# A graph layer's last 24 edge blocks: messages in halves, queued behind dense work, and dense work paced

## The chip, the cores and the metric

The kernel runs on one core of a Trainium2 chip. A core has five engines that work side by side, each through its own queue in order: TensorE (PE; matmuls; its weight loads are PEld in the profile), VectorE (DVE), ScalarE (ACT), GpSimd (POOL, which here only starts gathers) and SyncE (SP, which here only starts other transfers). The metric is the device time of one execution in microseconds (us); lower is better.

## The reference

A graph network layer over 8192 nodes with 256 channels and 131072 edges with 64 features. Edges come sorted by their destination.

```python
ea = edge_attr @ w_e + b_e
msg = relu(x[src] + ea)
agg = segment_sum(msg, dst, num_segments=N)
t = x + agg
h_local = bn(relu(t @ w1 + b1) @ w2 + b2 + x)
# attention with 4 heads inside groups of 32 nodes, on x
h_attn = bn(attention(x) + x)
out = h_local + h_attn
out = bn(out + relu(out @ m_w1 + m_b1) @ m_w2 + m_b2)
return layernorm(x + out)
```

All is float32. The edge part (`msg`, `agg`) and the attention depend on x alone; the dense part (w1, w2, m_w1, m_w2, layer norm) of a node needs the sums of all its edges.

## The kernel before, in words

**Edges** go in 128 blocks of 1024. A block is four groups (`NH`) of two columns of 128 edges (`TJ`). Its steps, with their lines:

- `gather` (L157): eight indirect DMAs on POOL, 128 rows of x each, into one of four buffers `xs`.
- `edge_products` (L208): edge features times w_e on PE. Each pair of groups (half a block) fills one tile `pe` of two PSUM banks; there are two such tiles, and the attention scores (L474) take the same two in turn.
- `edge_messages` (L229, L233): for each half, DVE adds `pe` and the gathered rows, then ACT takes the relu. There are three `msg` buffers.
- `edge_hot` (L241): one-hot columns of each edge's destination inside its group's window of 32 nodes, on DVE.
- `edge_sums` (L250, L263): PE sums messages by destination into tile `pw` (one buffer), ACT copies the sums to `ws`, DVE makes a second one-hot `oh2` (L267).
- `edge_place` (L278, L287): PE spreads the window sums over some 100 to 160 nodes, into a tile that shares the buffer of `pw`, and DVE adds them to the chunk's `xT`.
- `next_edges` (L190): DVE transposes the features of the block after next, and SP loads further ones.

**Nodes** go in 16 chunks of 512. `attention_front` and `attention_back` compute a chunk's attention ahead of time; `dense` (the layers at L546, the relus on ACT at L553 and L562, the scaled additions on DVE at L556 and L574, transposes at L583, layer norm at L589 to L601, the store at L606) starts when the last block that reaches the chunk has been placed. They are Python generators which yield after each step, with the step's cost in us as the writer estimates it. The second to last chunk's dense part goes in two halves, the last chunk's in four quarters of 128 nodes, on two streams.

**Order.** PE runs in the order in which the program states its matmuls. The order on DVE and ACT is chosen by a scheduler, except that `tc.issue_after(i)` puts what is stated inside it behind instruction `i` on the same engine. Up to block 103 two blocks go per round, with shares of dense work between. From block 104 (`TAIL`) a planner states the steps one by one. It keeps an estimated clock `t`; `came[i]` is the time at which it expects block i's gathers, `7.9 + 10.035 * (i + 1)`. In each turn it takes the first of these that is due: placing a block, its sums, products of the next block, messages; if none is due, `work.step` states one dense or attention step. Messages of a block stand behind the newest `ws` copy and the newest addition to `xT`. Products of a block come after the messages of the block before; the last block's two halves of products are stated by hand, one after the sums of block 126 and one after its placement.

Of the kernel before, what the change touches and what calls it, by code (L numbers as in the profile page):

```python
# [18 lines left out]
P = 128  # L19
# [5 lines left out]
NH = 4  # L25
# [16 lines left out]
TAIL = 104  # L42
AGG_ROWS = N + 2 * P
# [29 lines left out]
def gnn_kernel(ctx: ExitStack, tc: tile.TileContext, x, src, dst, edge_attr, w, out):  # L73
# [119 lines left out]
    pe_of, msg_of, oh_of, newest = {}, {}, {}, {}  # L193
# [25 lines left out]
    def edge_messages(b):  # L219

        xs = xs_of.pop(b)
        msg = msg_of[b] = epool.tile([P, NH, TJ, C], FP, name="msg", tag="msg", bufs=3)
        n = 2 if b < NB - 1 else 1
        for h in range(0, NH, 2):
            pe = pe_of.pop((b, h))
            for u in range(0, 2, n):
                hs = slice(h + u, h + u + n)
                for js in [slice(0, TJ)] if n == 2 or h + u < NH - 1 else [slice(j, j + 1) for j in range(TJ)]:
                    nc.vector.tensor_add(  # L229
                        msg[:, hs, js].rearrange("p u i c -> p i u c"), pe[:, js, u : u + n, :],  # L230
                        xs[:, hs, js].rearrange("p u i c -> p i u c"),
                    )
                    nc.scalar.activation(msg[:, hs, js], msg[:, hs, js], AF.Relu)  # L233
        between()
# [19 lines left out]

    def edge_sums(blocks):

        n = len(blocks)
        pw = pps.tile([P, 2, C], FP, name="pw", tag="pw", bufs=1)
        for i, b in enumerate(blocks):
            turns = [(h, j) for j in range(TJ) for h in range(NH)]  # L260
            group_sums(pw, i, b, sorted(turns) if b == NB - 1 else turns)
        ws = epool.tile([P, 2, C], FP, name="ws", tag="ws", bufs=2)
        newest["ws"] = nc.scalar.copy(ws[:, :n], pw[:, :n]).ins  # L263
# [269 lines left out]
    def dense(n0, st, pool, bank, a=0, z=CH, own=("h1", "m1", "zT", "y", "")):  # L533
# [18 lines left out]
        for o in range(KC):  # L552
            nc.scalar.activation(h1[:, o, :], layer(w1, KC, o, tT), AF.Relu, bias=v_("b1", o))  # L553
            yield 1.7 * part
        for o in range(KC):
            nc.vector.scalar_tensor_tensor(  # L556
                hA[:, o, :], layer(w2, KC, o, h1), s1[:, o : o + 1], hA[:, o, :], op0=ALU.mult, op1=ALU.add
            )
            yield 1.7 * part
        m1 = pool.tile([P, 2 * KC, w], FP, name="m1", tag=own[1])  # L560
        for o in range(2 * KC):
            nc.scalar.activation(m1[:, o, :], layer(mw1, KC, o, hA), AF.Relu, bias=v_("m_b1", o))  # L562
            yield 1.7 * part
# [9 lines left out]
        for o in range(KC):  # L573
            nc.vector.scalar_tensor_tensor(  # L574
                zT[:, o, :], layer(mw2, 2 * KC, o, m1), s3[:, o : o + 1], zT[:, o, :], op0=ALU.mult, op1=ALU.add
            )
# [66 lines left out]
    class Work:  # L643
# [5 lines left out]
        def __init__(self, n):  # L649
            self.streams = [[] for _ in range(n)]  # L650
            self.rest, self.turn, self.owed = [0] * n, 0, 0.0
            self.at, self.placed_at = [0.0] * n, 0.0

# [56 lines left out]
    with tc.manual_schedule(engines={PE}):  # L710
# [23 lines left out]
        for i, c, a, z in (  # L734
            (DENSE2, NCH - 2, 0, CH // 2), (DENSE, NCH - 2, CH // 2, CH), (DENSE2, NCH - 1, 0, P),
# [56 lines left out]
        t, p, m, s, l = came[b - 2] + 20, b, b, b - 2, b - 2  # L792
        added = dict((i, came[i] + 2.0) for i in range(b))
        summed_at, bank_free = {}, t
        work.at = [t] * len(work.streams)
        while l < NB:

            times = [1e9] * 4
            if l < s:
                times[0] = summed_at[l] + 1.5  # L800
            elif s < m:
                times[1] = max(added[s] + 1.2, bank_free)
                if s == NB - 1:
                    times[1] = max(came[s] + 2.2, bank_free)
            if p < NB - 1 and m == p:
                times[2] = added[p - 1]
            if m < p:
                times[3] = came[m]
            if t >= times[0]:
                edge_place(*sums)  # L810
                placed = l
                t += 0.75
                bank_free = work.placed_at = t + 0.7
                l += 1
                if l == NB - 1:
                    edge_products(l, [2])
                    edge_hot(l)
                    t += 1.0
                    p += 1
            elif t >= times[1]:  # L820
                sums = edge_sums([s])
                t += 1.2
                summed_at[s] = t
                s += 1
                if s == NB - 1:
                    edge_products(s, [0])
                    t += 1.0
            elif t >= times[2]:
                if p + 2 < NB:
                    gather(p + 2)  # L830
                edge_products(p)
                next_edges(p + 2)
                edge_hot(p)
                t += 2.1
                p += 1
            elif t >= times[3]:

                with ExitStack() as behind:
                    for i in newest.values():
                        behind.enter_context(tc.issue_after(i))  # L840
                    edge_messages(m)
                added[m] = max(t, came[m], added[m - 1] + 0.5) + 2.0
                m += 1
            elif l == s - 1 == NB - 1:
                t = times[0]
# [127 lines left out]
```

## Time and profile before

| what | value |
|---|---|
| median of 3 runs | 1315.99 us (1314.24 to 1318.11) |
| the profiled execution | 1315.85 us, span of its instructions 1314.1 us |
| PE busy | 1198.9 us (91%) |
| POOL busy | 975.3 us (74%), with 0.3 us to issue between two gathers |
| DVE, ACT busy | 803.9 us (61%), 592.0 us (45%) |
| last gather starts | 1289.26 us |
| last operation on DVE starts | 1309.12 us |
| mean TensorE clock granted | 0.964 of full speed |

How to read it: a timeline row gives start, length, engine, line, operation, output and inputs, how many instructions are merged, and in brackets the idle time of the engine ahead of it with what ended that. A windows row gives a stretch, its length, and for PE, PEld, DVE, ACT and POOL the busy us and the number of instructions, then the granted TensorE clock, the share of the DMA engines and GB/s. A waits row names who waited for whom, with the sum in us and the number of times. Every matmul on float32 shows as two rows of PE. Line numbers are those of the kernel before.

### The profile page before, as it was taken

How to read it: one execution, taken by the hardware profiler on the slowest of the kernel's cores; microseconds unless marked ns; L12 is line 12 of the kernel's file. 1: busy time of each engine (PE TensorE's matmuls, PEld its weight loads, DVE VectorE, ACT ScalarE, POOL GpSimd, SP SyncE). 2: the span in 40 equal slices, each digit the busy share in tenths (PEclk: the TensorE clock that was granted, in tenths of full speed). 3: DMA queues.
4: the chain of work that ended last, by engine and by line, in shares of the span. 5: the costliest groups of instructions: out<-in, count | busy, mean ns of one | idle time of the engine just before them, and what ended most of it. 6: DMA issues, size and time to landing. Idle time of an engine off the chain costs nothing.

```text
span 1314.1 us, 21073 instructions
## 1 busy us (share of the span) xinstructions
PE 1198.9 (91%) x7683; PEld 722.8 (55%) x7683; DVE 803.9 (61%) x1634; ACT 592.0 (45%) x850; POOL 975.3 (74%) x1032
## 2 busy tenths in 40 slices
PE   5987989999999989898997999889898999989986
PEld 3554646556565555555564555545555555555665
DVE  6567665757566565745746574565647558475663
ACT  2524444454545264443544444354454445453443
POOL 7777777777777777777777777777777777777772
PEclk8989999999999989898999999989899999999998
DMA  9999976677666666665767566576566567665741
GB/s 230 280 328 275 280 216 166 175 188 192 169 182 158 171 181 159 188 163 152 195 163 185 153 185 169 154 186 169 169 170 191 149 168 194 162 168 154 193 135 48
DMA packets 148922, 240.35 MB, mean 183 GB/s; under 512 B 27950, under 2 KB 112204, under 8 KB 148044
## 3 DMA queue, kind: packets, MB, share of 16 engines
q0 software_dynamic: 49152, 134.28, 38.6%
q1 hardware_dynamic: 98572, 104.65, 29.4%
q8 instruction: 62, 1.02, 0.3%
q14 instruction: 48, 0.39, 0.1%
q10 hardware_dynamic: 1088, 0.00, 0.0%
HBM read 222.06 MB, written 16.78 MB: 182 GB/s over the span
## 4 chain that ended last, share of the span: by engine, by line
POOL 34%; PE 31%; issue 16%; DMA 9%; DVE 8%; ACT 2%; SPq 0%; DVEq 0%; POOLq 0%; ACTq 0%
POOL xs L157 34%; PE at L546 8%; DMA xs<-xb,srci 6%; PE pe L208 6%; PE at L443 3%; PE pw L250 3%; PE pe L203 2%; PE at L524 2%; DVE msg L229 2%; PE l L278 1%; DVE bd L504 1%; PE at L512 1%; PE at L457 1%; DMA xb<-xp 1%; DVE eaT L190 1%
## 5 line engine op out<-in xcount | busy, mean ns | idle before, releaser
L157 POOL DMA_INDIRECT xs<-xb,srci x864 | 819.1, 948 | 263.2 <-issue 247.7
L233 ACT ACTIVATE msg<-msg 128x1024 f32<-128x1024 f32 (+1 forms) x259 | 270.0, 1046 | 401.4 <-DVE msg L229 397.4
L229 DVE TENSOR_TENSOR msg<-pe,xs 128x1024 f32<-128x1024 f32 (+1 forms) x259 | 306.6, 1207 | 196.5 <-PE pe L208 91.2
L208 PE MATMUL pe<-we,eaT 64*128 64x256 f32 x2048 | 270.3, 401 | 13.5 <-ACT pr L484 9.8
L208 PEld LDWEIGHTS pe<-we,eaT 64*128 64x128 f32 x2048 | 195.4, 194 | 117.9 <-issue 62.8
L157 POOL DMA_INDIRECT xs<-in_x_dram,srci x144 | 138.8, 964 | 43.9 <-issue 40.8
L250 PE MATMUL pw<-msg,oh 128*32 128x256 f32 x2048 | 129.8, 385 | 1.2 <-ACT msg L233 0.8
L546 PE MATMUL at<-hA,mw 128*128 128x512 f32 (+2 forms) x320 | 125.8, 520 | 4.5 <-DVE hA L556 4.3
L443 PE MATMUL at<-xT,inT 128*128 128x512 f32 x256 | 121.8, 602 | 3.2 <-ACT xT L433 3.2
L546 PE MATMUL at<-m,mw 128*128 128x512 f32 (+2 forms) x320 | 119.4, 517 | 0.0
L190 DVE STREAM_TRANSPOSE eaT<-ea 128x512 f32<-128x512 f32 x128 | 90.0, 703 | 22.0 <-PE pe L208 18.6
L250 PEld LDWEIGHTS pw<-msg,oh 128*32 128x32 f32 x2048 | 59.9, 110 | 63.6 <-issue 22.8
L278 PEld LDWEIGHTS l<-oh,ws 128*128 128x128 f32 x512 | 73.7, 195 | 27.3 <-issue 21.4
L278 PE MATMUL l<-oh,ws 128*128 128x160 f32 (+4 forms) x512 | 85.9, 308 | 1.8 <-ACT ws L263 1.7
L546 PEld LDWEIGHTS at<-hA,mw 128*128 128x128 f32 x320 | 55.1, 192 | 53.4 <-issue 41.2
L546 PEld LDWEIGHTS at<-m,mw 128*128 128x128 f32 x320 | 55.7, 192 | 48.0 <-issue 44.8
L443 PEld LDWEIGHTS at<-xT,inT 128*128 128x128 f32 x256 | 46.9, 191 | 57.4 <-issue 47.6
L446 ACT ACTIVATE qk<-at,vec 128x512 f32<-128x512 f32 x64 | 43.8, 685 | 73.7 <-PE at L443 73.6
L546 PE MATMUL at<-xT,w 128*128 128x512 f32 (+2 forms) x160 | 66.3, 551 | 8.8 <-DVE xT L287 8.8
L562 ACT ACTIVATE m<-at,vec 128x512 f32<-128x512 f32 (+2 forms) x80 | 47.9, 599 | 58.5 <-PE at L546 58.0
L546 PE MATMUL at<-h,w 128*128 128x512 f32 (+2 forms) x160 | 65.3, 532 | 9.4 <-ACT oT L519 7.0
L241 DVE TENSOR_TENSOR oh<-iota_n,rel 128x128 f32<-128x128 f32 x256 | 57.6, 279 | 18.2 <-PE pw L250 14.8
(111 smaller groups left out, 1200.7 us busy)
## 6 DMA issues: line engine op xcount, KB each, us to landing
ea<-in_edge_attr_dram SPq DMA_DIRECT2D x512, 128.0 KB
xs<-xb,srci POOLq DMA_INDIRECT x864
xn<-in_x_dram SPq DMA_DIRECT2D x16, 512.0 KB
out_dram<-y SPq DMA_DIRECT2D x14, 512.0 KB
xp<-in_x_dram SPq DMA_DIRECT2D x10, 512.0 KB
xb<-xp SPq DMA_DIRECT2D x10, 512.0 KB
xp<-in_x_dram SPq DMA_DIRECT2D x3, 1024.0 KB
xb<-xp SPq DMA_DIRECT2D x3, 1024.0 KB
```

The source lines that it names most:

```text
L157: nc.gpsimd.indirect_dma_start(out=xs[:, h, j, :], out_offset=None, in_=x if b < NX else xb[:, :], in_offset=bass.IndirectOffsetOnAxis(ap= ...
L190: nc.vector.transpose(eaT, ea[:, QR:].rearrange("p (g d) -> p g d", d=ED)[:, :, :QR])
L208: nc.tensor.matmul(pe[:, i, u, :], eaT[rows, h + u], we[rows, :], start=(b >= NX), stop=True, skip_group_check=True)
L229: nc.vector.tensor_add(msg[:, hs, js].rearrange("p u i c -> p i u c"), pe[:, js, u : u + n, :], xs[:, hs, js].rearrange("p u i c -> p i u c"),
L233: nc.scalar.activation(msg[:, hs, js], msg[:, hs, js], AF.Relu)
L241: nc.vector.tensor_tensor(oh[:, ts], iota_n[:, None, :WN].to_broadcast([P, TB // 2, WN]), rel[:, b, ts, None].to_broadcast([P, TB // 2, WN ...
L250: nc.tensor.matmul(pw[h * WN : (h + 1) * WN, i, :], oh_of[b][:, h * TJ + j, :], msg_of[b][:, h, j, :], start=(j == 0), stop=(j == TJ - 1), ...
L278: nc.tensor.matmul(l2[:, k, at : at + wn], ws[:, i, k * P : (k + 1) * P], oh2[:, i, :wn], start=(i == 0 and k == 0), stop=(i == last), ski ...
L443: nc.tensor.matmul(ps, inT[:, k, o * P : (o + 1) * P], xT[:, k, :], start=(k == 0), stop=(k == KC - 1))
L446: nc.scalar.activation(qk[:, o, :], ps, AF.Identity, bias=v_("in_b", o))
L546: nc.tensor.matmul(ps, wt[:, k, o * P : (o + 1) * P], act[:, k, :], start=(k == 0), stop=(k == nk - 1))
L562: nc.scalar.activation(m1[:, o, :], layer(mw1, KC, o, hA), AF.Relu, bias=v_("m_b1", o))
```

## The change

It touches the last 24 blocks alone, with five edits.

1. Products, messages and sums go by halves of a block. The planner keeps for each of the three which block and which half is next; products of half k of a block become due when the message of half k of the block before is expected to be added. The first half of a block's sums can be stated before its second half's messages. The last block goes the same way; its sums go as three groups and then one.
2. Dense work is added to what messages stand behind: the newest relu (L553, L562) on ACT and the newest scaled addition (L556, L574) on DVE. The attention's own scaled addition isn't among them.
3. Between the expected times of block 115 and block 124 (`came[115]` to `came[124]`), dense and attention steps are stated only as credit allows, which grows by 0.42 us per us.
4. The second half of chunk 14's dense part goes as two quarters.
5. The planner's estimates change: shorter times for placements and sums, and an order of turns in which messages come ahead of products.

```diff
+SHARE = 0.42
...
-    def edge_messages(b):
+    def edge_messages(b, pairs=range(0, NH, 2)):
...
-        for h in range(0, NH, 2):
+        for h in pairs:
...
+    def some_sums(b, groups):
+
+        if b not in pw_of:
+            pw_of[b] = pps.tile([P, 2, C], FP, name="pw", tag="pw", bufs=1)
+        group_sums(pw_of[b], 0, b, [(h, j) for h in groups for j in range(TJ)])
...
-            nc.scalar.activation(h1[:, o, :], layer(w1, KC, o, tT), AF.Relu, bias=v_("b1", o))
+            newest["relu"] = nc.scalar.activation(h1[:, o, :], layer(w1, KC, o, tT), AF.Relu, bias=v_("b1", o)).ins
...
-            nc.vector.scalar_tensor_tensor(
+            newest["dense"] = nc.vector.scalar_tensor_tensor(
...
         def step(self, t, until):
 
+            if self.paced_from <= t < self.paced_to:
+                self.credit += SHARE * (t - max(self.seen, self.paced_from))
+                self.seen = t
+                if self.credit < -0.02:
+                    return min(until, t - self.credit / SHARE)
...
                     elif d > 0:
                         t += d
+                        if self.paced_from <= t:
+                            self.credit -= d
...
-            (DENSE2, NCH - 2, 0, CH // 2), (DENSE, NCH - 2, CH // 2, CH), (DENSE2, NCH - 1, 0, P),
+            (DENSE2, NCH - 2, 0, CH // 2), (DENSE, NCH - 2, CH // 2, 3 * P), (DENSE, NCH - 2, 3 * P, CH),
+            (DENSE2, NCH - 1, 0, P),
...
+        p, m, s = [b, 0], [b, 0], [b - 2, 0]
+        added = dict(((i, k), came[i] - 1.2 + 2.5 * k) for i in range(b) for k in range(2))
...
+        work.paced_from, work.paced_to = came[115], came[124]
...
+            if p[0] < NB and (p[0] - 1, p[1]) < tuple(m):
+                times[2] = added[p[0] - 1, p[1]]
+            if tuple(m) < tuple(p):
+                times[3] = came[m[0]] - 2.5 * (1 - m[1])
...
             elif t >= times[3]:
 
                 with ExitStack() as behind:
                     for i in newest.values():
                         behind.enter_context(tc.issue_after(i))
-                    edge_messages(m)
...
+                    edge_messages(m[0], (2 * m[1],))
+                added[tuple(m)] = max(t, came[m[0]] - 2.5 * (1 - m[1])) + 1.3
+                onward(m)
+            elif t >= times[2]:
+                i, k = p
+                if not k and i + 2 < NB:
+                    gather(i + 2)
+                edge_products(i, (2 * k,))
+                if k:
+                    next_edges(i + 2)
+                else:
+                    edge_hot(i)
+                t += 1.0
+                onward(p)
```

More of the change, by code (lines that the diff above doesn't have):

```diff
@@ L190, in edge_transpose @@
         nc.vector.transpose(eaT, ea[:, QR:].rearrange("p (g d) -> p g d", d=ED)[:, :, :QR])
-    pe_of, msg_of, oh_of, newest = {}, {}, {}, {}
+    pe_of, msg_of, oh_of, pw_of, newest = {}, {}, {}, {}, {}
     def edge_products(b, pairs=range(0, NH, 2)):
@@ L561, in dense @@
         for o in range(2 * KC):
-            nc.scalar.activation(m1[:, o, :], layer(mw1, KC, o, hA), AF.Relu, bias=v_("m_b1", o))
+            newest["relu"] = nc.scalar.activation(m1[:, o, :], layer(mw1, KC, o, hA), AF.Relu, bias=v_("m_b1", o)).ins
             yield 1.7 * part
@@ L573, in dense @@
         for o in range(KC):
-            nc.vector.scalar_tensor_tensor(
+            newest["dense"] = nc.vector.scalar_tensor_tensor(
                 zT[:, o, :], layer(mw2, 2 * KC, o, m1), s3[:, o : o + 1], zT[:, o, :], op0=ALU.mult, op1=ALU.add
-            )
+            ).ins
             yield 3.4 * part
@@ L811, in gnn_kernel @@
                 placed = l
-                t += 0.75
+                t += 0.6
                 bank_free = work.placed_at = t + 0.7
                 l += 1
[L815 to L819, printed above, removed]
-            elif t >= times[1]:
[L821 to L835, printed above, removed]
+            elif t >= times[1]:
+                i, k = s
+                last = range(NH - 1, NH) if i == NB - 1 else range(NH // 2, NH)
+                some_sums(i, last if k else range(last.start))
+                t += 0.14 * TJ * (len(last) if k else last.start)
+                if k:
+                    sums = edge_sums([i])
+                    summed_at[i] = t
+                onward(s)
             elif t >= times[3]:
```

45 lines of the change are left out of this document (22 added, 23 removed).

## The prediction

> **What bounds the kernel now.** I read the page first, then the windows over the last 250 us, then the timelines of POOL, DVE and PE there, and last the waits.
>
> ```profile
> span 1314.1 us, 21073 instructions
> PE 1198.9 (91%) x7683; PEld 722.8 (55%) x7683; DVE 803.9 (61%) x1634; ACT 592.0 (45%) x850; POOL 975.3 (74%) x1032
> ```
>
> The profiled execution took 1315.85 us, 1.75 us more than its span; the median of the three runs is 1315.99, so the sum below stands for the median as well.
>
> POOL sets a floor. Its gathers follow each other without a stall to the last:
>
> ```profile
> 1288.01 0.95 POOL L157 DMA_INDIRECT xs<-xb,srci  x1 [0.30 <-issue]
> 1289.26 0.94 POOL L157 DMA_INDIRECT xs<-xb,srci  x1 [0.30 <-issue]
> 1286.75 3.00 DMA xs<-xb,srci
> ```
>
> 0.95 + 0.30 us a gather, eight to a block, is 10.0 us a block, and the last one lands at about 1289.26 + 3.0 = 1292.3. Nothing in the diff makes a gather cheaper or earlier. So the change can only act on the 22 us behind 1292, or push what stands there back.
>
> ```profile
> 1064.00:1130.00 66.00, 62.45 (x434) 35.82 (x436) 44.65 (x92) 31.85 (x49) 49.97 (x53) 1.00 0.67 178
> 1130.00:1200.00 70.00, 65.83 (x414) 38.28 (x407) 44.68 (x89) 32.03 (x49) 53.03 (x56) 1.00 0.62 166
> 1200.00:1250.00 50.00, 47.10 (x316) 31.94 (x316) 32.01 (x71) 20.26 (x34) 37.90 (x40) 1.00 0.69 174
> 1250.00:1289.00 39.00, 32.71 (x259) 24.33 (x256) 23.55 (x52) 16.54 (x31) 29.51 (x32) 0.93 0.48 132
> 1289.00:1314.00 25.00, 16.72 (x131) 13.87 (x130) 9.26 (x26) 9.21 (x24) 0.94 (x1) 0.91 0.09 26
> ```
>
> The columns are the stretch, its length, and busy us of PE, PEld, DVE, ACT and POOL. PE is busy 175.4 of the 186 us from 1064 to 1250 (94%): in the last 24 blocks the bound is PE, not POOL. It is behind the gathers there, and catches up only at the end:
>
> ```profile
> 1148.88 0.95 POOL L157 DMA_INDIRECT xs<-xb,srci  x1 [0.31 <-issue]
> 1161.81 2.34 DVE L229 TENSOR_TENSOR msg<-pe,xs 128x1024 f32<-128x1024 f32 x2
> 1272.19 1.23 DVE L229 TENSOR_TENSOR msg<-pe,xs 128x1024 f32<-128x1024 f32 x1 [1.70 <-DMA xs<-xb,srci]
> ```
>
> Counting eight gathers and two messages to a block, the first two rows belong to block 113: its last rows landed near 1152, its messages ran ten us later. At block 125 (third row) DVE waits for the landing: the lag is gone. So PE has just enough room to reach the last gather without a backlog. PE idle time added before 1250 is not hidden by POOL; it arrives at the end, less what the waits of the last blocks give back.
>
> **The change part by part.** Matmul work is the same: 8 products, 8 sums, 2 placements a block, the same dense columns. What moves is who stands behind whom.
>
> *Halves.* Products of half a block go into one of the two double banks, and that bank is free once the message (L229) two halves earlier has read it. Before, both halves' messages stand side by side on DVE, so PE meets this wait once a block; now twice, with dense work between.
>
> *Messages behind dense work.* The newest dense operation on DVE and on ACT joins what a message must stand behind. DVE takes its instructions in order, so a message now waits until the dense matmul named ahead of it has left PE, and PE's next products wait for that message. The built order of the changed kernel shows it: of the 45 gaps between successive messages in DVE's order of these blocks, 19 held nothing before and 8 hold nothing now.
>
> The durations for this, from before:
>
> ```profile
> L229 DVE TENSOR_TENSOR msg<-pe,xs x46: 1189/1215/1225, 1068.6 to 1282.1; 128x1024 f32<-128x1024 f32 x46
> 1077.01 0.75 DVE L574 SCALAR_TENSOR_TENSOR zT<-at,s,zT 128x512 f32<-128x512 f32 x1 [0.41 <-PE at L546]
> 1280.40 0.34 DVE L574 SCALAR_TENSOR_TENSOR zT<-at,s,zT 128x128 f32<-128x128 f32 x1
> 1073.58 0.56 DVE L287 TENSOR_TENSOR xT<-l,xT 128x224 f32<-128x224 f32 x2
> 1261.55 2.00 PE L546 MATMUL at<-m,mw 128*128 128x128 f32 x16
> 1095.50 0.65 PE L278 MATMUL l<-oh,ws 128*128 128x144 f32 x4
> 1099.51 2.27 PE L208 MATMUL pe<-we,eaT 64*128 64x256 f32 x16 [1.64 <-DVE msg L229]
> PE pe L208 <- DVE msg L229: 2.7, 2, 1.6
> ```
>
> A typical turn, late: PE ends the first half of a 128-wide m_w2 layer; its result is on DVE about 0.25 us later (the 2.00 against 1.77 that 16 rows take at the pace of the groups around), then zT 0.34, then message 1.22: 1.8 us until the products may start. PE's cover is the second half of that layer, 0.9 us. Wait: 0.9 us. With 512 columns it is 0.25 + 0.75 + 1.22 = 2.2 under a cover of 1.7, wait 0.5. The dearest place is the softmax of a chunk:
>
> ```profile
> 1083.28 0.69 DVE L490 TENSOR_REDUCE mx<-pr 128x16 f32<-128x512 f32 x1 [1.87 <-ACT pr L484]
> 1084.41 1.22 DVE L229 TENSOR_TENSOR msg<-pe,xs 128x1024 f32<-128x1024 f32 x1
> 1086.57 1.19 DVE L229 TENSOR_TENSOR msg<-pe,xs 128x1024 f32<-128x1024 f32 x1
> 1091.93 2.14 DVE L504 STREAM_TRANSPOSE bd<-pr 32x512 f32<-32x512 f32 x3
> 1095.11 1.28 DVE L589 TENSOR_TENSOR y<-at,xn 128x512 f32<-128x512 f32 x2
> ```
>
> Before, two messages slip in between the first pieces of the softmax; then 11.7 us of DVE pass without one, and PE waits the 1.64 us of the L208 row above. In the changed order no message stands inside it, some 12 us pass from mx on, with the next message behind the layer norm's sums; PE has about 10 us of other work meanwhile, wait 2.8 us, 1.2 more.
>
> I went through the built orders of PE, DVE and ACT this way, turn by turn with such rows, from where they part (1067 us) to the last gather. **Products behind messages:** 15 waits of 0.9 us on average, 14, against the 2.7 that before shows: **+11**. Bounds: 0 (every message finds its dense operation done) and 46 x 0.9 = 41. I take the count. **Scores behind messages:** scores (L474) use the same banks; two chunks' scores now come directly behind a placement: 0.25 + 0.75 (zT) + 0.5 (xT) + 1.22 less the 0.6 of the placement is 2.1 each, **+4** (bounds 0 and 5).
>
> **Given back.** With PE late, some waits that before has vanish:
>
> ```profile
> PE at L546 <- DVE xT L287: 4.9, 5, 2.7
> PE at L583 <- DVE zT L574: 2.9, 2, 2.3
> PE at L546 <- DVE hA L556: 1.8, 1, 1.8
> ```
>
> 9.6 us, half of which is chain that stays: **-4.5** (bounds -9.6 and 0).
>
> **The end.** Before, block 126 is placed ahead of the last landing and the final chain is short:
>
> ```profile
> 1294.62 1.09 PE L250 MATMUL pw<-msg,oh 128*32 128x256 f32 x16
> 1296.29 0.69 PE L278 MATMUL l<-oh,ws 128*128 128x96 f32 x4 [0.57 <-ACT ws L263]
> 1297.39 0.71 PE L546 MATMUL at<-xT,w 128*128 128x128 f32 x4 [0.42 <-DVE xT L287]
> ```
>
> Now products, sums, placement and dense of block 126 and of 127 both lie behind the last landing, with block 127's messages behind 126's dense. Each placement has two bare round trips on PE (ws, xT: about 0.6 and 0.7 here, since nothing fills them), each start of a 128-wide dense piece two or three of 0.3 us, one message turn 0.9 to 1.3: **+4** (bounds 0 and 7).
>
> **Clock.** PE granted at half speed shows once in these blocks:
>
> ```profile
> 1279.89:1283.30 3.41, 1.44 (x13) 1.20 (x11) 2.07 (x4) 1.06 (x1) 2.50 (x4) 1.00 0.31 96
> 1283.30:1286.72 3.42, 3.10 (x19) 1.35 (x21) 2.29 (x8) 1.59 (x3) 2.54 (x3) 0.50 0.41 117
> 1286.72:1290.13 3.41, 3.41 (x16) 2.33 (x16) 0.61 (x2) 0.13 (x1) 2.77 (x3) 0.50 0.56 147
> ```
>
> After a stretch in which PE worked 1.44 of 3.41 us (42%) the next two ran at 0.50. Each such stretch takes 1.7 us of PE's work when PE is the bound. Waits of 2 to 3 us, as above, make them likelier; I expect one to two events of one or two stretches: **+4** (bounds 0 and 9). The Trainium skill, "TensorE: Matmul & The Clock Gate", Part 1: The HAM clock gate, has the clock halve after at least one idle window of about 3.4 us; by that rule taken literally, no wait worked out here is long enough and this term is 0, the sum 4 us less. The trace speaks for the milder trigger: 42% busy sufficed.
>
> **Held back dense, and the rest.** From the due time of block 115 to that of block 124, some 90 us, dense steps get 0.42 of the time by the planner's account. Against a PE that is behind, this holds back little that would have run; where it does, it adds idle of the kind counted. I cost it at 0; cover is PE's own backlog, and without it up to 5 us. Cutting chunk 14's second half into two pieces doubles its small ACT and DVE operations (0.3 to 0.4 us each, some ten on either engine); ACT is busy 20.26 of 50 us there, so 0, or 2 if they fall into the chain. Gathers wait for a message four blocks back: 40 us of buffers against a lag that I put at 15 to 22 us by block 113, so 0; past about 28 us each further us moves POOL.
>
> Sum: 11 + 4 - 4.5 + 4 + 4 = +18.5, so 1315.85 + 18.5 = **1334.4 us**.
>
> **The rivals.**
> *Absorbed (13%).* The added waits fall where PE would have waited anyway, and the planner's pacing keeps work for the gaps: 6.3 us of idle in the row of 1250:1289 and the 9.6 above take up most of +15; with +4 at the end and no clock events: 1320, between 1316 and 1325. For it: the lag in before does shrink by ten us from block 113 to 123. Against it: that catching-up is already spent there.
>
> *Faster (10%).* If each half's dense operation is done when its gathers land, halves let sums of a block start half a block earlier, and the paced dense work fills 1279.9 to 1283.3, so that the half clock doesn't come. Then sums of 126, products of 127 and the placement (2.35, 2.08, 1.17, 1.47 us on PE from 1284.03 on, at half clock) run at full speed and lie before the landing; the last sums start at their messages' end, 1293.4 instead of 1294.62, and one m_w1 step fewer lies behind the placement (0.45 twice): 1315.85 - 1.2 - 0.9 = 1313.7, with a second clock event avoided at the very end 1311. It decides at the lag: block 127's first message must start within a us of its landing. Against it: PE at 94%, so there is no gap to fill earlier on.
>
> ```profile
> 1284.03 2.35 PE L250 MATMUL pw<-msg,oh 128*32 128x256 f32 x16
> 1286.31 2.08 PE L208 MATMUL pe<-we,eaT 64*128 64x256 f32 x8
> 1288.32 1.17 PE L278 MATMUL l<-oh,ws 128*128 128x96 f32 x4
> 1289.41 1.47 PE L208 MATMUL pe<-we,eaT 64*128 64x256 f32 x8
> ```
>
> *Run away (12%).* The clock falls again and again (five or more stretches, 9 us), the lag passes 28 us and gathers stall for want of buffers: 1334 + 5 + 6 = 1345 or more.
>
> **How the numbers follow.** Forecast 65%, 1325 to 1344; absorbed 13%, faster 10%, run away 12%. 0.3% is 4 us, about what a measurement of this kernel can tell from no change. Faster by more than that: 9%. Within it: 1% of the faster case and 4% of the absorbed: 5%. Slower: 86%. The range leaves out the faster case and most of the run away one: 1317 to 1345.
>
> **What would show it.** Right: the last gather still at 1289; messages of blocks 112 to 127 some 12 to 20 us behind their landings; block 127's first message not before 1296; PE waiting for messages (L229's successor) 10 us or more longer in total between 1067 and 1289; several stretches at clock 0.50. Wrong: messages of the last blocks waiting for DMA, as at 1272 before; PE's busy share above 94% there; or the clock at 1.00 throughout with the end at 1329, which would strike the clock's term alone.

## The result, and the profile after

The changed kernel takes **1353.48 us** (median of 4 runs, 1350.44 to 1356.75) beside 1316.01 for the kernel before (4 runs): ratio 1.0285, 95% interval 1.0256 to 1.0313. It is slower by 37.5 us where 18.5 were forecast, and it lies above the range. The profiled execution took 1353.57 us.

The first lines of the page of after, which answer to the first two shown of before:

```profile
span 1351.8 us, 21180 instructions
PE 1228.7 (91%) x7731; PEld 733.1 (54%) x7731; DVE 804.0 (59%) x1640; ACT 595.9 (44%) x859; POOL 976.8 (72%) x1032
```

The share of PE is 91% in both, which looks like no change. The microseconds tell more: PE is busy 1228.7 - 1198.9 = 29.8 us longer, and not busy 123.1 us against 115.2, 7.9 longer. So most of the 37.7 us between the spans is not waiting. It is matmul time, though the matmul instructions are the same but for the 48 rows of chunk 14's extra piece.

The windows of after, for the stretches shown of before up to the last gathers:

```profile
1064.00:1130.00 66.00, 58.97 (x376) 32.51 (x376) 40.01 (x85) 26.51 (x41) 50.14 (x53) 0.97 0.66 170
1130.00:1200.00 70.00, 64.16 (x355) 34.43 (x352) 36.19 (x75) 26.96 (x41) 49.44 (x53) 0.95 0.53 143
1200.00:1250.00 50.00, 46.42 (x236) 23.85 (x237) 26.96 (x51) 17.29 (x24) 34.94 (x37) 1.00 0.57 150
1250.00:1289.00 39.00, 35.59 (x248) 25.40 (x246) 23.89 (x58) 17.07 (x34) 29.01 (x32) 1.00 0.67 179
```

From 1200 to 1250 PE is as busy as before (46.42 against 47.10 us, clock 1.00 in both) and finishes 236 rows instead of 316. Rows differ in size, so the count alone does not show slower work; the groups below do. A window from 1064 to 1289 says it in a line for each kernel, first before, then after:

```profile
1064.00:1289.00 225.00, 208.08 (x1409) 130.37 (x1408) 144.89 (x304) 100.69 (x160) 170.41 (x180) 0.99 0.63 165
```

```profile
1064.00:1289.00 225.00, 205.14 (x1206) 116.19 (x1206) 127.05 (x266) 87.83 (x137) 163.53 (x173) 0.98 0.60 159
```

Idle time of PE there went from 16.9 to 19.9 us, 3 more; work done fell by 203 rows of 1409. Which operation became dear shows in the groups by line over the same 225 us. The columns are the count of rows, then busy us and mean ns of one, then the idle time ahead of them and what ended it. First before, then after:

```profile
L250 PE MATMUL pw<-msg,oh 128*32 128x256 f32 x400 | 29.8, 395 | 1.2 <-ACT msg L233 0.8 <-DVE xT L287 0.4
```

```profile
L209 PE MATMUL pe<-we,eaT 64*128 64x256 f32 x326 | 47.6, 412 | 10.3 <-DVE msg L232 8.4 <-ACT pr L494 1.9
L253 PE MATMUL pw<-msg,oh 128*32 128x256 f32 x336 | 43.3, 397 | 2.8 <-ACT msg L236 2.8
L556 PE MATMUL at<-xT,w 128*128 128x128 f32 (+2 forms) x48 | 14.6, 427 | 1.0 <-DVE xT L297 1.0
L484 PE MATMUL pe<-qk 64*128 64x128 f32 x64 | 5.3, 315 | 3.8 <-DVE msg L232 3.8
```

The sums (L250 before, L253 after) take 29.8 us for 400 rows and 43.3 for 336. The mean of one row is the same, 395 and 397 ns. So no matmul became longer; **fewer of them run at once**. From 1064 us to the end both kernels do all 416 rows of their sums, first before, then after:

```profile
L250 PE MATMUL pw<-msg,oh 128*32 128x256 f32 x416 | 30.9, 395 | 1.2 <-ACT msg L233 0.8 <-DVE xT L287 0.4
L253 PE MATMUL pw<-msg,oh 128*32 128x256 f32 x416 | 54.2, 395 | 2.8 <-ACT msg L236 2.8
```

In that stretch PE is busy 224.8 us before and 256.2 after, 31.4 more, and idle 25.3 and 31.6, 6.3 more. The sums alone account for 23.3 of the 31.4, and the products (50.3 and 55.8 us for 384 rows) for 5.5. The timeline of PE shows how, before:

```profile
1140.00 1.07 PE L250 MATMUL pw<-msg,oh 128*32 128x256 f32 x16
1141.00 2.00 PE L208 MATMUL pe<-we,eaT 64*128 64x256 f32 x16
```

and after:

```profile
1130.41 1.06 PE L253 MATMUL pw<-msg,oh 128*32 128x256 f32 x8
1131.41 1.13 PE L209 MATMUL pe<-we,eaT 64*128 64x256 f32 x8
1132.47 1.06 PE L253 MATMUL pw<-msg,oh 128*32 128x256 f32 x8
```

Sixteen rows of sums, a whole block, hold PE from 1140.00 to 1141.00. Eight rows, half a block, hold it from 1130.41 to 1131.41, the same 1.0 us. A sum writes 32 columns of the array (128\*32), one column group for each group of edges. In the single records before, four rows start within 0.02 us of each other, once every 0.216 us; after, two. A half holds only two of the four edge groups, so only two column groups have work. The block's sums cost 2.0 us instead of 1.0, and 21 blocks go this way. At three places early in the tail both halves of a block stand with nothing between them, and there the sixteen rows take 1.0 us again (the next row starts at 1073.37), although their order is that of the halves. So it is the work between the halves that costs, and not the new order:

```profile
1072.35 1.09 PE L253 MATMUL pw<-msg,oh 128*32 128x256 f32 x16
```

The products lose less, and in another way: eight rows take 1.06 us (1131.41 to 1132.47), two halves 2.12, where 16 rows before took 1.92 (1141.00 to the next row at 1142.92). Two rows run at a time in both, but the first step of each run takes 0.32 us instead of 0.216, and halves make twice as many runs.

The backlog grew accordingly. The table gives how far the second message of a block starts behind the landing of the block's last rows (start of its last gather plus 2.8 us), in us:

| kernel | block 107 | 113 | 117 | 126 | first message of 127 starts at |
|---|---|---|---|---|---|
| before | 8 | 11 | 5 | 0 | 1289.8 |
| after | 11 | 32 | 31 | 28 | 1329.7 |

At block 113 the gathers began to stall for buffers. Rows of POOL and of DVE in after:

```profile
1150.45 0.95 POOL L158 DMA_INDIRECT xs<-xb,srci  x1 [0.30 <-issue]
1186.51 0.95 POOL L158 DMA_INDIRECT xs<-xb,srci  x1 [4.99 <-DVE oh L277]
1299.97 0.94 POOL L158 DMA_INDIRECT xs<-xb,srci  x1 [0.30 <-issue]
```

```profile
1185.05 1.19 DVE L232 TENSOR_TENSOR msg<-pe,xs 128x1024 f32<-128x1024 f32 x1
1329.73 1.28 DVE L232 TENSOR_TENSOR msg<-pe,xs 128x512 f32<-128x512 f32 x2
```

The first POOL row is the last gather of block 113, the first DVE row its second message, 34.6 us later; 0.3 us behind that message's end POOL goes on, after 5 us idle. (The row names the one-hot L277, which DVE does just behind; the buffer was the message's.) The last gather starts at 1299.97, 10.7 us later than before. That cost nothing: its rows landed near 1303 and their message began at 1329.73, when PE came to it. From that message to the end of the span it is 22.1 us, and before 24.3 (from 1289.80). The end itself did not lengthen. All of the loss is backlog brought along.

### The profile page after: what moved, and what is told of

The parts are those of the page before. It is cut to its first block, busy times and chain, and to the rows that moved or that the text cites. A ratio compares the mean times of both kernels' runs of the same rounds, so it can differ in the third digit from the quotient of the medians.

```text
span 1351.8 us, 21180 instructions
## 1 busy us (share of the span) xinstructions
PE 1228.7 (91%) x7731; PEld 733.1 (54%) x7731; DVE 804.0 (59%) x1640; ACT 595.9 (44%) x859; POOL 976.8 (72%) x1032
## 3 DMA queue, kind: packets, MB, share of 16 engines
q1 hardware_dynamic: 98588, 104.65, 28.9%
## 4 chain that ended last, share of the span: by engine, by line
PE 42%; POOL 26%; issue 13%; DMA 8%; DVE 8%; ACT 3%; SPq 0%; DVEq 0%; ACTq 0%; POOLq 0%
POOL xs L158 26%; PE at L556 13%; PE pe L209 9%; PE pw L253 5%; DMA xs<-xb,srci 5%; PE at L453 4%; DVE msg L232 3%; PE at L534 3%; PE l L288 3%; PE pe L204 2%; PE at L467 2%; DMA xs<-in_x_dram,srci 1%; DMA ea<-in_edge_attr_dram 1%; PE at L522 1%; ACT msg L236 1%
## 5 line engine op out<-in xcount | busy, mean ns | idle before, releaser
L209 PEld LDWEIGHTS pe<-we,eaT 64*128 64x128 f32 x2048 | 190.9, 191 | 132.1 <-issue 65.3
L253 PE MATMUL pw<-msg,oh 128*32 128x256 f32 x2048 | 152.8, 385 | 2.8 <-ACT msg L236 2.8
L556 PE MATMUL at<-hA,mw 128*128 128x512 f32 (+2 forms) x336 | 127.9, 506 | 3.8 <-DVE hA L566 3.7
L556 PE MATMUL at<-m,mw 128*128 128x512 f32 (+2 forms) x336 | 119.5, 500 | 0.0
L253 PEld LDWEIGHTS pw<-msg,oh 128*32 128x32 f32 x2048 | 68.1, 110 | 72.9 <-issue 24.4
L288 PEld LDWEIGHTS l<-oh,ws 128*128 128x128 f32 x512 | 74.3, 196 | 26.8 <-issue 19.9
L556 PEld LDWEIGHTS at<-hA,mw 128*128 128x128 f32 x336 | 56.0, 192 | 54.5 <-issue 44.0
L556 PEld LDWEIGHTS at<-m,mw 128*128 128x128 f32 x336 | 56.4, 192 | 48.4 <-issue 46.7
L584 DVE SCALAR_TENSOR_TENSOR zT<-at,s,zT 128x512 f32<-128x512 f32 (+2 forms) x42 | 26.1, 621 | 81.4 <-PE at L556 80.7
L556 PE MATMUL at<-h,w 128*128 128x512 f32 (+2 forms) x168 | 67.2, 523 | 7.6 <-ACT oT L529 6.1
L556 PE MATMUL at<-xT,w 128*128 128x512 f32 (+2 forms) x168 | 68.9, 545 | 4.0 <-DVE xT L297 3.9
```

The lines of the kernel that those rows point to most:

```text
L209: nc.tensor.matmul(pe[:, i, u, :], eaT[rows, h + u], we[rows, :], start=(b >= NX), stop=True, skip_group_check=True)
L253: nc.tensor.matmul(pw[h * WN : (h + 1) * WN, i, :], oh_of[b][:, h * TJ + j, :], msg_of[b][:, h, j, :], start=(j == 0), stop=(j == TJ - 1), ...
L288: nc.tensor.matmul(l2[:, k, at : at + wn], ws[:, i, k * P : (k + 1) * P], oh2[:, i, :wn], start=(i == 0 and k == 0), stop=(i == last), ski ...
L556: nc.tensor.matmul(ps, wt[:, k, o * P : (o + 1) * P], act[:, k, :], start=(k == 0), stop=(k == nk - 1))
```

## The experiments

The theory **S** (sums): halves of the sums keep PE busy twice as long, and that is the larger part of what the forecast missed. The rivals: messages behind dense operations cost far more than the +15 forecast; or the pacing starves PE. In all experiments the whole of the computation is done.

The four edits, each alone or together, as they are named below. **Sums whole** (from after): all sums of blocks 104 to 126 are stated with the second half.

```diff
-                some_sums(i, last if k else range(last.start))
-                t += 0.14 * TJ * (len(last) if k else last.start)
+                if i == NB - 1:
+                    some_sums(i, last if k else range(last.start))
+                if k or i == NB - 1:
+                    t += 0.14 * TJ * (len(last) if k else last.start) * (1 if i == NB - 1 else 2)
```

**Messages free** (from after): they stand behind placement and sums alone, as in before.

```diff
-                    for i in newest.values():
+                    for i in (newest["ws"], newest["xT"]):
```

**Sums apart** (from before): one dense or attention step, where one is ready, between a block's first two groups and its last two.

```diff
-            group_sums(pw, i, b, sorted(turns) if b == NB - 1 else turns)
+            if apart and b < NB - 1:
+                group_sums(pw, i, b, [g for g in turns if g[0] < NH // 2])
+                apart()
+                group_sums(pw, i, b, [g for g in turns if g[0] >= NH // 2])
+            else:
+                group_sums(pw, i, b, sorted(turns) if b == NB - 1 else turns)
...
-                sums = edge_sums([s])
-                t += 1.2
+                ahead = []
+                sums = edge_sums([s], lambda: ahead.append(work.step(t, t)))
+                t = max([t, *ahead]) + 1.2
```

**Messages behind dense** (from before): whole messages also stand behind the newest relu and scaled addition.

```diff
-            nc.scalar.activation(h1[:, o, :], layer(w1, KC, o, tT), AF.Relu, bias=v_("b1", o))
+            newest["relu"] = nc.scalar.activation(h1[:, o, :], layer(w1, KC, o, tT), AF.Relu, bias=v_("b1", o)).ins
...
-            nc.vector.scalar_tensor_tensor(
+            newest["dense"] = nc.vector.scalar_tensor_tensor(
```

### First set: lost to the chip

From after: sums whole (e1), messages free (e2), no pacing (e3, `work.paced_from, work.paced_to = 1e9, 0.0`); from before: sums apart (e4).

> The changed kernel with the sums of blocks 104 to 126 stated whole again, once both halves' messages are stated; all else as changed. Theory S (half a block's sums take PE 1.0 us, as long as a whole block's, so 1.0 us more a block): 23 us of PE come back, the gathers no longer stall, 1325 to 1336 us. Theory O (all of the loss is messages queued behind dense work): no more than a few us, 1348 to 1354. Theory P (the loss is the dense work held back): 1350 to 1354.

> The changed kernel with messages behind the newest ws copy and the newest addition to xT alone, as before the change; halves, sums in halves and pacing stay. S: PE is still given 1.0 us more a block, 1333 to 1345 us. O alone: back to 1316 to 1320. P alone: no change, 1350 to 1354.

> The changed kernel without the pacing of dense work. P: 1335 or less. S and O: PE has no room that the pacing could have left unused, so no gain; dense work stated earlier puts messages further behind and the gathers stall more, 1350 to 1365.

> The kernel before, where for blocks 102 to 126 a dense or attention step (if one is ready) is stated between the sums of the first two groups and those of the last two; messages, products and order of all else as before. S: about 1.0 us more PE a block, 24 less the 8 to 10 us by which PE catches up before the last gather: 1326 to 1334 us. O and P: nothing that they blame is here, 1315 to 1319.

Measured: 2005.2, 2003.1, 2013.2 and 1963.5 us, and the kernel before itself took 1970.67 on that chip (13 runs); ratios 1.0175, 1.0131, 1.0217 and 0.9964. In the trace of e4, DVE has 39 gaps of more than 8 us between two instructions, ACT 38, POOL 32 and PE 12; in that of before, on another chip, ACT has 6 and the others none. Rows of e4, its page and its waits:

```profile
span 1967.8 us, 21076 instructions
PE 1419.9 (72%) x7683; PEld 804.3 (41%) x7683; DVE 806.2 (41%) x1634; ACT 593.8 (30%) x850; POOL 972.0 (49%) x1032
```

```profile
POOL xs L157 <- DVE msg L229: 597.5, 66, 20.1
```

With PE busy 72% and waits of up to 20 us, PE is not the bound there, and a question about PE's work can't be asked. All that follows from e4 (interval 0.9931 to 0.9996) is that parting the sums cost nothing where PE has room.

### Second set: parts taken off after

f1 is after with sums whole; g1 is after with messages free; f2 has both.

> The changed kernel with the sums of blocks 104 to 126 stated whole, all else as changed; once more, since the first chip held every engine still some 35 times for about 15 us, in the kernel before as well (1971 us), and PE was busy 72% only. On a chip that gives about 1316 us for the kernel before, S: 23 us of PE come back and the gathers no longer stall, 1325 to 1336 us. O alone: 1348 to 1354.

> The changed kernel with sums whole and with messages behind the newest ws copy and addition to xT alone; products and messages by halves, pacing and smaller pieces stay. S and O together are the whole loss if this comes to 1311 to 1319 us. If S is all of it, this equals f1 (both 1316 to 1320). If pacing or halves of products cost of themselves (P), it stays above 1325.

> The changed kernel with messages behind the newest ws copy and the newest addition to xT alone; sums stay in halves. Sums whole took 11.7 us off the changed kernel and freeing messages then 15.7 more. If the two add (S and O independent): 1353.5 - 15.7 = 1338 us. If S carries more while O is gone, because PE has no other wait to hide its 23 us behind: up to 1349. O alone: 1326 or less, as f2.

| kernel | median, us | before beside it | ratio (95%) | slower by, us | page: span | PE busy | not busy |
|---|---|---|---|---|---|---|---|
| before | 1316.01 | | | | 1314.1 | 1198.9 | 115.2 |
| after | 1353.48 | 1316.01 | 1.0285 (1.0256 to 1.0313) | 37.5 | 1351.8 | 1228.7 | 123.1 |
| f1 | 1341.78 | 1315.44 | 1.0202 (1.0185 to 1.0219) | 26.3 | 1337.5 | 1209.3 | 128.2 |
| g1 | 1343.98 | 1315.09 | 1.0220 (1.0203 to 1.0237) | 28.9 | 1342.5 | 1225.7 | 116.8 |
| f2 | 1326.11 | 1315.44 | 1.0078 (1.0061 to 1.0094) | 10.7 | 1324.7 | 1205.4 | 119.3 |

Sums whole gave back 11.2 us, and not the whole of what the forecast had missed: S as I put it for f1 (1325 to 1336) was too simple. The page of f1 and its groups over 1064 to 1289 tell why:

```profile
span 1337.5 us, 21179 instructions
PE 1209.3 (90%) x7731; PEld 725.3 (54%) x7731; DVE 804.6 (60%) x1640; ACT 596.6 (45%) x859; POOL 975.8 (73%) x1032
```

```profile
L209 PE MATMUL pe<-we,eaT 64*128 64x256 f32 x336 | 49.5, 415 | 20.5 <-DVE msg L232 18.0 <-ACT pr L494 2.5
L253 PE MATMUL pw<-msg,oh 128*32 128x256 f32 x336 | 24.0, 394 | 3.6 <-ACT msg L236 3.6
```

The same 336 rows of sums fall from 43.3 to 24.0 us, 19.3 less. But the products' wait for messages rises from 8.4 to 18.0, 9.6 more. 19.3 - 9.6 = 9.7, near the 11.2. The long sums had been covering waits for messages; with PE faster, the waits show. Not all of them come from the message order: in f2, where messages are free again, the products still wait 11.1 us. Taking both off gives 37.5 - 10.7 = 26.8, more than 11.2 + 8.6: one cost hid part of the other. Read from the table, whole sums are worth 11.2 us while messages stand behind dense work and 28.9 - 10.7 = 18.2 once they are free; free messages are worth 8.6 with sums in halves and 26.3 - 10.7 = 15.6 with whole sums.

### Third set: parts put on before, alone

So each part was added to the kernel before by itself: sums apart (g2), messages behind dense (g3), and the pacing with chunk 14's extra piece (g4).

```diff
+            if self.paced_from <= t < self.paced_to:
+                self.credit += SHARE * (t - max(self.seen, self.paced_from))
...
-            (DENSE2, NCH - 2, 0, CH // 2), (DENSE, NCH - 2, CH // 2, CH), (DENSE2, NCH - 1, 0, P),
+            (DENSE2, NCH - 2, 0, CH // 2), (DENSE, NCH - 2, CH // 2, 3 * P), (DENSE, NCH - 2, 3 * P, CH), (DENSE2, NCH - 1, 0, P),
...
+        work.paced_from, work.paced_to = came[115], came[124]
```

> The kernel before with a dense or attention step stated between the sums of the first two groups and those of the last two, where one is ready. S: 1.0 us more PE for each block where a step comes between, up to 24, less the 8 to 10 us by which PE catches up: 1322 to 1334 us. Without S: 1315 to 1318.

> The kernel before with its whole messages also behind the newest relu and the newest scaled addition of the dense part. O without halves: 1320 to 1332 us, with messages of the last blocks 5 us or more behind their landings. If O needs halves (both messages at once let PE meet the wait once a block): 1315 to 1319.

> The kernel before with the pacing of dense work and the second half of chunk 14 in two quarters; no halves, nothing else behind dense work. P (pacing costs PE time): 1322 us or more. Otherwise within 3 us of 1315.5; faster by up to 3 if the paced work fills the gap ahead of 1283 us and the clock isn't halved there.

| kernel | median, us (before: 1315.09) | ratio (95%) | slower by, us | from 1064 us on: PE busy against before, us | not busy |
|---|---|---|---|---|---|
| g2 sums apart | 1332.53 | 1.0135 (1.0118 to 1.0152) | 17.4 | +18.9 | -3.9 |
| g3 messages behind dense | 1324.67 | 1.0080 (1.0063 to 1.0097) | 9.6 | +2.0 | +4.9 |
| g4 pacing, extra piece | 1316.27 | 1.0007 (0.9997 to 1.0017) | 1.2 | -0.6 | +1.4 |

The last two columns are from the profiled executions (spans 1329.1, 1321.0 and 1314.9), from 1064 us to the end, where before has 224.8 us busy and 25.3 not. Ahead of 1064 the kernels do the same work, and yet PE's busy time there is 4.6 us less in g3 than in before (969.4 and 974.0), so totals over the whole page would mislead. The two columns show two costs of different kinds. Page, groups over 1064 to 1289 and timeline of PE of g2:

```profile
span 1329.1 us, 21076 instructions
PE 1214.3 (91%) x7683; PEld 725.7 (55%) x7683; DVE 801.7 (60%) x1634; ACT 592.8 (45%) x850; POOL 976.1 (73%) x1032
```

```profile
L250 PE MATMUL pw<-msg,oh 128*32 128x256 f32 x366 | 42.5, 391 | 2.7 <-DVE xT L292 2.7
```

```profile
1147.87 1.06 PE L250 MATMUL pw<-msg,oh 128*32 128x256 f32 x8
1148.85 1.98 PE L551 MATMUL at<-hA,mw 128*128 128x512 f32 x4
1150.77 1.06 PE L250 MATMUL pw<-msg,oh 128*32 128x256 f32 x8
1151.76 2.00 PE L208 MATMUL pe<-we,eaT 64*128 64x256 f32 x16
```

Each half of the sums holds PE for 1.0 us (1147.87 to 1148.85, 1150.77 to 1151.76), with a dense step between. g2 has whole products, whole messages and the old message order, and yet its sums are like those of after: 42.5 us for 366 rows where before has 29.8 for 400. All of its loss is busy time of PE, and from 1064 us on the sums have 16.4 us of it (47.3 against 30.9): some 16 blocks found a step to put between, where after parts 21. In g3 PE mostly waits more, 4.9 us of the 6.9 between the spans. Its waits for messages from 1064 to 1289:

```profile
PE pe L474 <- DVE msg L229: 3.1, 2, 2.1
PE pe L208 <- DVE msg L229: 2.7, 2, 1.6
```

The scores wait 3.1 us, where before shows no such wait. The products wait 2.7 us, exactly as before: with whole messages the dense order alone doesn't make them wait longer. g4 can't be told from before, so no cost of pacing and piece is seen when they are added to before; whether the pacing costs or helps where PE is as late as in after stays open.

### Fourth set: the halves of products and messages

m1 is f2 with products' due times and messages for whole blocks as well. What is left of the change then is the planner's estimates and turns, the pacing and the extra piece.

```diff
-                    edge_messages(m[0], (2 * m[1],))
+                    if m[0] >= HB:
+                        edge_messages(m[0], (2 * m[1],))
+                    elif m[1]:
+                        edge_messages(m[0])
```

with `HB = 128`; further kernels let halves begin late, at block 121 (h2, k2, m2) or 112 (h3), to learn whether halves cost only where PE is behind; h4 is f2 without the pacing; h1 and k1 are the same kernel as m1.

> k1's kernel a third time, for a chip whose engines don't stand still: products, messages and sums whole; the changed planner's due times, turns, pacing and smaller pieces stay. H (halves of products and messages cost the rest): 1314 to 1318 us. T (due times, turns or pacing cost it): 1323 or more.

m1 took 1318.95 us beside 1315.36: 1.0034 (1.0021 to 1.0046), 3.6 us slower. That is just above the range given for H and far below that for T. So whole products and messages are worth 10.7 - 3.6 = 7.1. Waits of the products for messages in f2, then in m1, from 1064 to 1289:

```profile
PE pe L209 <- DVE msg L232: 11.1, 6, 4.2
PE pe L211 <- DVE msg L234: 2.7, 1, 2.7
```

In m1 the wait for messages is back at what before has, 2.7, though one wait of 5.1 us behind a layer norm's operation on DVE comes in its place. The products' own time falls by about 1.7 us (from 1064 us on 55.9 us for 384 rows in f2, 53.1 for 376 in m1). How the 7.1 divides between the two is not shown.

The other seven ran on chips as slow as the first (before took 1962.6, 2022.3 and 2029.5 us there), and answer nothing:

> f2 with products and messages whole again as well (only the last block's sums still go as three groups and one); the changed planner's due times, turns, pacing and smaller pieces stay. f2 stood 10.7 us above before. If halves of products and messages cost that (H): 1314 to 1318 us. If the new due times and turns or the pacing cost it (T): 1323 or more.

> f2 with halves of products and messages from block 121 on alone, where PE has caught up; whole before that. H says that halves cost where PE is behind: nothing here, and block 126's sums and the last products can be ahead of the last landing: 1312 to 1316 us. T: 1323 or more.

> f2 with halves of products and messages from block 112 on. In f2 the messages' lag rises by 8 us at block 107 and by 10 at block 113, each beside a softmax. If halves cost at each softmax: half of 10.7 is left, 1319 to 1322 us. If it is a cost of every block: 1320 to 1323. If it is the first softmax alone: 1314 to 1318.

> f2 without the pacing: halves of products and messages and the smaller pieces alone. If pacing is what costs (P): 1316 or less. If it costs nothing with PE behind: within 3 us of f2's 1326. If it spares the messages some waiting, as dense work stated later stands behind them: 1329 to 1338.

> h1's kernel once more, on a chip whose engines don't stand still: products, messages and sums whole; the changed planner's due times, turns, pacing and smaller pieces stay. H (halves cost the rest): 1314 to 1318 us. T (due times, turns or pacing cost it): 1323 or more.

> h2's kernel once more: halves of products and messages from block 121 on alone. H: 1312 to 1316 us, the lag gone by block 125 and no half clock between 1283 and 1290. T: 1323 or more.

> m1's kernel (1318.95) with halves of products and messages from block 121 on. H says that halves cost where PE is behind, and from 121 on it has caught up: no dearer than m1, and if the last block's first sums start nearer to their landing, down to 1314. If halves cost in every block alike, 7.1 us over 23 blocks: 2 us more, 1321.

Ratios: h1 1.0130, h2 1.0097, h3 1.0107, h4 1.0152; k1 1.0075, k2 1.0072; m2 1.0152. The kernel of m1, 1.0034 where PE is the bound, is 1.0130 and 1.0075 on two of those chips; the late halves were never measured where they could tell.

**The account.** Added alone to before: sums apart 17.4, messages behind dense 9.6. The rest of the change, f2: 10.7, of which halves of products and messages 7.1 and due times, turns, pacing and piece 3.6. Together 17.4 + 9.6 + 10.7 = 37.7 us, against 37.5 measured. That it comes out so close is partly luck: g2 parts fewer blocks than after, and inside the changed kernel the same two parts are worth 11.2 to 18.2 and 8.6 to 15.6. Compared like with like, the sums are the largest part each time. No version beat the kernel before on the chips where PE is the bound.

## Why the prediction was wrong, point by point

- **The bound.** Right: PE bounds these blocks, and PE time added before 1250 came out at the end. The point was read, and then only waits were looked for.
- **"Matmul work is the same: 8 products, 8 sums, 2 placements a block."** This is the step that failed. The count is the same, the time is not: two column groups at a time instead of four make 1.0 us more of sums in each parted block, 23.3 us of PE in all, a term that the prediction put at nothing. g2, which parts the sums with dense steps and leaves the rest as in before, loses 17.4 us, about as much as the whole forecast loss. The row that could have said it stood in the prediction, 1294.62 with 1.09 us for sixteen rows of sums, beside 1099.51 with 2.27 us for sixteen rows of products. Sixteen rows of 256 columns in half the time mean that more of them run side by side. The products' 0.2 us a block (5.5 us in all by their groups) were left out by the same sentence.
- **Products behind messages, +11.** The mechanism was right. The wait in after rose from 2.7 to 8.4, only +5.7, because the long sums covered some of it; with sums whole (f1) it is 18.0, +15.3. Freeing the messages as well (f2) leaves 11.1, so 6.9 of the 15.3 come from the dense order; with products and messages whole too (m1) it is 2.7 again, so the other 8.4 go with the halves. Both of the causes named were at work. Messages behind dense alone (g3) cost 9.6 us, near the 10.5 forecast for waits (+11 and +4 less 4.5), but that is a coincidence, since the products don't wait longer in g3 and no halves are in it.
- **Scores behind messages, +4.** L484 waits 3.8 us for messages, where before its group shows none: right.
- **Given back, -4.5.** The three waits of 4.9, 2.9 and 1.8 us are 1.0, 0.2 and none in after: -8.4, larger, as it had to be with PE so late. All in all, PE's idle time in the 225 us rose by 3 us: 5.7 + 3.8 - 8.4, and 2.0 for sums that wait for the relu (2.8 against 0.8).
- **The end, +4.** Wrong, as far as it can be compared: 22.1 us from the last block's first message to the end, 24.3 before. Dense work was left over for the round trips that I had counted as bare, as the timeline of PE in after shows between the layers of the last block (xT,w) and behind its placement:

```profile
1334.51 0.71 PE L556 MATMUL at<-hA,mw 128*128 128x128 f32 x4
1335.06 0.67 PE L288 MATMUL l<-oh,ws 128*128 128x96 f32 x4
1336.15 0.71 PE L556 MATMUL at<-xT,w 128*128 128x128 f32 x4 [0.42 <-DVE xT L297]
1336.70 0.61 PE L556 MATMUL at<-hA,mw 128*128 128x128 f32 x4
```

- **Clock, +4.** Three stretches of after ran at half clock while there were blocks left. The windows of after show them, each with the stretch ahead of it, and at the end a stretch of little work that no fall followed:

```profile
1101.43:1104.84 3.41, 0.88 (x8) 0.69 (x8) 3.41 (x12) 0.90 (x1) 2.71 (x3) 1.00 0.93 218
1104.84:1108.25 3.41, 3.41 (x14) 1.31 (x11) 2.44 (x7) 2.69 (x4) 2.49 (x4) 0.50 1.00 282
1162.87:1166.28 3.41, 1.44 (x21) 1.22 (x22) 3.01 (x3) 1.32 (x2) 2.69 (x3) 1.00 0.35 100
1166.28:1169.70 3.42, 2.83 (x22) 2.36 (x22) 0.00 (x0) 3.33 (x9) 2.50 (x4) 0.50 0.38 104
1169.70:1173.11 3.41, 3.41 (x18) 1.39 (x16) 1.58 (x5) 1.67 (x3) 2.50 (x4) 0.50 0.35 108
1183.35:1186.76 3.41, 1.57 (x10) 0.40 (x8) 3.15 (x11) 1.18 (x2) 0.26 (x1) 1.00 0.00 0
1186.76:1190.17 3.41, 2.79 (x22) 1.68 (x22) 1.64 (x6) 2.40 (x4) 2.59 (x3) 1.00 0.28 77
```

  Half of the busy time in the three is 4.8 us; before lost 3.3 in its two, which after doesn't have. Net some +1.5: the events came, the kernel before had its own to set against them.
- **Pacing and pieces, 0.** g4 agrees on the kernel before (1.2 us, interval with no change in it).
- **The rivals.** *Run away* named what happened: a lag past 28 us, stalled gathers, 1345 or more; 12% for it was too little. But the cause was another (not the clock), and the price of 6 us for the stall was wrong, for the late gathers still landed 27 us ahead of their message. *Absorbed* was right that much would hide, only it was the added work that hid the added waits.
- **The signs.** "Last gather still at 1289" failed by 10.7 us, and messages were 25 to 33 us behind from block 113 on instead of 12 to 20: the signs showed the size at once. The sign that waits for messages would rise by 10 us or more failed too, narrowly (+5.7 and +3.8, 9.5 together): with so late a kernel and so small a growth in waits, the time had to be in PE's work. Two signs held: block 127's first message came after 1296 (at 1329.7), and three stretches ran at clock 0.50.

## What to carry to other kernels

Before an operation is cut into parts, look in its timeline row for how many instructions share one step of time: where matmuls of few columns run side by side, a part that keeps only some of the column groups takes as long as the whole. Compare busy microseconds and counts per operation, not shares, because an engine that is the bound shows 91% whether it works well or badly. And take costs off and put them on alone: what comes off a changed kernel (11.2 for the sums) can be less than what went on (17.4) while another part of the change waits in the same place.

## What the runs showed of the hardware

- Half of a block's sums, eight rows on two column groups of 32, takes the 1.0 us of sixteen rows on four. The Trainium skill, "TensorEngine Tiling (Array Packing)", section Key Properties, has it that tiles operate independently and can run matmuls in parallel; the trace agrees (four rows start within 0.02 us), and shows the other side of it: one tile's rows still follow each other every 0.216 us, whether four tiles are in use or two.
- In after, the granted clock halved after stretches of 3.41 us in which PE was busy 0.88 and 1.44 us (26% and 42%), and not after one of 1.57 us (46%). After 2.83 us busy (83%) at half clock it stayed at half for one more stretch. The Trainium skill, "TensorE: Matmul & The Clock Gate", section Part 1: The HAM clock gate, speaks of an idle window; in none of these stretches was PE idle, so here less sufficed. The busy share alone doesn't decide it, though, and the prediction's "42% busy sufficed" is no rule: earlier in before the clock halved after 1.69 us busy (49%; half clock from 389.01) and not after 1.44 us (42%). What decides between these shares is open.

```profile
385.60:389.01 3.41, 1.69 (x18) 1.05 (x16) 2.07 (x11) 3.31 (x8) 2.50 (x4) 1.00 0.88 203
389.01:392.42 3.41, 2.46 (x10) 1.63 (x11) 2.84 (x6) 1.93 (x4) 2.77 (x3) 0.50 0.85 274
474.35:477.76 3.41, 1.44 (x7) 0.67 (x5) 2.29 (x7) 3.15 (x4) 2.69 (x3) 1.00 0.64 167
477.76:481.17 3.41, 2.85 (x10) 1.50 (x11) 3.28 (x9) 3.41 (x6) 2.60 (x3) 1.00 0.90 199
```

- On three chips the same kernel before took 1963 to 2029 us instead of 1315 to 1316, with gaps of more than 8 us on DVE, ACT and POOL 32 to 39 times in the one execution whose gaps were counted (e4). What makes them was not found.
